# Idle transposes at the start, one product kept in PSUM, and weights moved by a graph, in a two-layer graph network

## The chip, the core and the metric

The kernel runs on one core of a Trainium2 chip. The metric is the device time of one execution in microseconds, and the median of several executions is compared. The engines are called as in the profile: PE (TensorE, matrix products), DVE (VectorE), ACT (ScalarE), POOL (GpSimd) and SP (SyncE, which here only issues DMA transfers). Each engine works through its own queue in order, and waits at an instruction until what that instruction needs is there.

## What is computed

There are 16 graphs of 1024 nodes with 256 features, one 1024x1024 adjacency matrix, and two layers:

```
# layer 0
h   = relu(layernorm(x))                    # x: 16 x 1024 x 256
A   = symmetric weights from the channel mean of h (abs, tanh)
g   = relu(einsum('bcn,bnm->bcm', h^T, adj * A) * para)
q   = g^T;  k, v = split(h @ kv_w)          # 4 heads of 64
x1  = x + softmax(q k^T * scale) v
# layer 1
h   = relu(layernorm(x1))
agg = A_hat @ h                             # normalised adjacency
y1  = relu(batchnorm(agg @ W1^T + b1))      # statistics over all 16 graphs
y2  = batchnorm(y1 @ W2^T + b2)             # the same
out = x1 + y2
```

Each batchnorm needs the statistics of all graphs before any value of it can be finished, so the program has three stages one after the other: attention of all graphs with the first product of layer 1 beside it, the second product of layer 1 for all graphs, and then the output of all graphs.

## The kernel before, in words

All data is float32. A tile is 128 partitions by some columns; a graph's 1024 nodes are 8 tiles (`NT`), its 256 features are 2 chunks (`CC`). In the part that runs, `layers(False)`, the order of the instructions on each engine is the order in which the program issues them (`layers(True)`, a version with shifted exponents for extreme inputs, is built too and not run here). That order is written with Python generators: `weave` takes one step of a main sequence and then one of each side sequence, `islice` takes so many steps, `double` takes two steps at a time. `run` works a sequence to its end.

**The start** (lines 1179 to 1200). `load_x(0)` (line 173) fetches graph 0 in two transfers of 512 KB on SP's queue; behind them stand the key and value weights (`kvw`) and the first pieces of the adjacency matrix (`load_adj`). `Norm` makes h tile by tile: statistics on DVE, the reciprocal root on POOL, a shift on DVE, then one ACT instruction per tile (`relu`, line 341). `transposed` (line 385) turns four tiles of h for one feature chunk into a PSUM bank with four PE transposes, and ACT copies the bank out (line 399). `keys_values` (line 643) makes k and v from it: the `pk` products. `differences` and `weigh` make the weights w of the graph products: per piece two ACT instructions `abs` (line 480), one `tanh` (line 488), and one multiplication with adj on DVE (line 467). `plain_queries` are the graph products (`pg`). All of these PSUM banks come in turn from one pool of three (`bank`, line 164).

**The attention stage** (`attention`, line 1086) is a loop of steps. A step issues the scores of two node tiles (`sc`, 8 PE instructions, into one of two PSUM buffers each), ACT makes their exponentials p (line 935), DVE adds these up (`acc`), and one step later PE multiplies p with v (`o`). Between these, PE gets background work: `background(b)` yields pieces with a cost, and a step takes pieces until `done` reaches `due`. The background of graph b's attention makes keys, values and queries of graph b+1, and the aggregation and hidden product of graph b-1. The weights of graph 2 are begun in graph 0's background, in `prepare(2, ...)` (lines 811 to 816): for each of two feature chunks up to three slots of `weigh` (an even slot is a multiplication of the piece before and the `abs` of the next, an odd slot is a `tanh`), beside v products, then the transposes of that chunk. Graph 1's background then goes on with them: one slot beside each of four `pk` products (line 852), then two slots beside each product of `queries(2)` (line 855).

**The second product** (`second`, line 1208). `graph(b, ...)` (line 1333) makes the product of graph b in seven block products of 4 PE instructions each (`m1` to `m7`, line 1328), which ACT and DVE combine into two tiles `y2_b_0` and `y2_b_1` that stay in SBUF to the end. `ahead_of(b + 1)` is taken between them: relu of the next graph's input on ACT, the combinations t1 and t2 on POOL, and the load of the input after that. The pair t1, t2 lies in the tile `both` for the first and last graph, else in the tags of `y2_15`. Between graphs `load_x1` (line 1243) fetches x1 of graph 0, 1, 2, ..., as far as there is room: three in the pool `xp`, four in the input buffers `yin`, one in `both`, so eight.

**The output** (lines 1444 to 1469). Per graph: ACT applies the batchnorm's scale and shift, 32 PE transposes turn y2 into rows (`pt`), DVE adds them onto x1 (line 1464), POOL issues two DMA writes of 512 KB, and one more x1 is fetched: graphs 8 to 10 into the tiles y2_0 to y2_2 whose turn is over, the others into buffers of earlier x1, which come free when their output has been written.

Of the kernel before, what the change touches and what calls it, by code (L numbers as in the profile page):

```python
# [10 lines left out]
F32 = mybir.dt.float32  # L11
# [12 lines left out]
def gnn_two_layers_kernel(  # L24
# [72 lines left out]
    def layers(shifted):  # L97
# [74 lines left out]

        def load_x(b):
            xs[b] = p3.tile([P, NT, C], F32, tag="x", name=f"x_{b}")
            for half in range(2):
                t = slice(half * NT // 2, (half + 1) * NT // 2)
                nc.sync.dma_start(
                    out=xs[b][:, t], in_=x[b].rearrange("(t p) c -> p t c", p=P)[:, t]
                )
# [202 lines left out]

        TOP = -1.0

        def transposed(b, k, halves=range(NH)):

            h = hs["a", b]
            if 0 in halves:
                ht = p3.tile([P, N], F32, tag="ht", name=f"ht_{b}_{k}")
                hts.setdefault(b, []).append(ht)  # L390
            ht = hts[b][k]
            for g in halves:
                pt = bank(f"htp_{b}_{k}_{g}")
                for j in range(FB // P):
                    t = g * (FB // P) + j
                    nc.tensor.transpose(
                        pt[:, j * P : (j + 1) * P], h[:, t, k * P : (k + 1) * P], ident
                    )
                nc.scalar.copy(ht[:, g * FB : (g + 1) * FB], pt)  # L399

        def squares(b):

# [86 lines left out]
                yield 0.0  # L489

        AHEAD = 6

        def quarters(tag, b):

# [311 lines left out]
        def prepare(b, products):  # L806


            w = weighers[b]
            yield from islice(products, 1)  # L810
            if b == 2:
                for k in range(CC):
                    yield from weave(islice(products, 3), (0, islice(w, AHEAD // 2)))
                    yield TOP
                    transposed(b, k)
# [13 lines left out]
        def background(b):  # L829

            if b == 0:
                differences(1)
                for k in range(CC):
                    yield TOP
                    transposed(1, k)
# [12 lines left out]
            before = hidden(b - 1)  # L848
            gather = aggregate(b - 1)
            if b + 1 < B:  # L850
                w, products, norm = weighers[b + 1], keys_values(b + 1), normed(b - 1)
                yield from weave(islice(products, 4), (0, islice(w, 4)))
                if b == 1:
                    load_later()
                yield from weave(queries(b + 1), (0, double(w)), (9, islice(norm, 5)))
                yield next(gather)
                yield from weave(products, (0, norm))
            else:
                yield from weave(endings.pop(), (2, normed(b - 1)))
# [295 lines left out]
        with st:  # L1155
            if shifted:
                for b in range(B):
                    if b > 0:
                        load_x(b)
                    run(Norm(b, True).all())  # L1160
                    differences(b)
                    for k in range(CC):
                        transposed(b, k)
                    run(islice(weighers[b], AHEAD))
                    run(weave(plain_queries(b), (0, weighers[b])))
                    if b == 0:
                        run(degrees(), graph())
                        load_later()
                    run(keys_values(b))
                    shifted_attention(b)  # L1170
                    norm = Norm(b, False)
                    run(norm.all())
                    keep(b)
                    if b == B - 1:
                        attn.close()
                        turns.append(second(kind))
                    run(aggregate(b), hidden(b))
            else:
                norm = Norm(0, True)
                norm.stats(0, 1)  # L1180
                norm.scale(0, 2)
                for t in range(2, NT, 2):
                    norm.stats(t, t + 1)
                    norm.shift(t - 2, 2)
                    norm.relu(t - 2, t - 1)
                    norm.scale(t, 2)
                norm.shift(NT - 2, 2)
                norm.relu(NT - 2, NT - 1)
                products = keys_values(0)

                for k in range(CC):
                    transposed(0, k, (0,))
                run(islice(products, 2))
                for k in range(CC):
                    transposed(0, k, (1,))
                differences(0)
                run(weave(products, (0, islice(weighers[0], AHEAD))))
                load_x(1)
# [9 lines left out]
    def second(kind):  # L1208
# [34 lines left out]
        def load_x1():  # L1243


            b = len(xos)
            name = f"xo_{kind}_{b}"
            HT = NT // 2
            if not 8 <= b < 11:
                pool, tag = ((xp, "xo"), (io, "yin"), (wp, "both"))[(b % 11 > 2) + (b % 11 > 6)]  # L1250
                xo = pool.tile([P, NT, C], F32, tag=tag, name=name)
                halves = [xo[:, :HT, :], xo[:, HT:, :]]
            else:
                halves = [
                    yp.tile([P, HT, C], F32, tag=f"y2_{b - 8}_{i}", name=f"{name}_{i}")
                    for i in range(2)
                ]
            for i in range(2):
                nc.sync.dma_start(out=halves[i], in_=by_rows(x1_d[b], i))
            xos.append(halves)  # L1260

        with st:
# [34 lines left out]

            def second_steps(b):

                if 0 < b < B - 1:  # L1300
                    pair = [
                        yp.tile([P, JH, FB], F32, tag=f"y2_{B - 1}_{i}", name=f"t{i}_{kind}_{b}")
                        for i in range(2)
                    ]
                else:
# [27 lines left out]
            def graph(b, ahead):  # L1333

                b11, t3, b21, b22 = inputs(b)
                y2.append(
                    [
                        yp.tile([P, N], F32, tag=f"y2_{b}_{k}", name=f"y2_{kind}_{b}_{k}")
                        for k in range(CC)
                    ]  # L1340
                )
# [34 lines left out]
            def ahead_of(b):  # L1376
# [15 lines left out]
                        load_y(2 * b + 2 + i)  # L1392
                yield

            stats2 = wp.tile([P, CC, B * NH, 6], F32, name="stats2")
            mv2 = wp.tile([P, CC, 2], F32, name="mv2")
            affs = []
# [28 lines left out]
            yield  # L1426
            yp = st.enter_context(tc.tile_pool(name=f"yp_{kind}", bufs=1, reuse_waits="tile"))
            xp = st.enter_context(tc.tile_pool(name=f"xp_{kind}", bufs=3))
            for b in range(B):
                graph(b, ahead_of(b + 1))  # L1430
                if b in (1, 3, 5, B - 2, B - 1):
                    for _ in range(1 + b // (B - 2)):
                        load_x1()
                if kind == "f" and b == B // 2:
# [97 lines left out]
```

## Time and profile before

| | us |
|---|---|
| median of 3 runs | 2499.18 (2499.15 to 2500.88) |
| the profiled execution, its own time | 2498.36 |
| its span, first to last instruction | 2496.6 |
| PE busy | 2436.2 |
| DVE busy | 1882.5 |
| ACT busy | 1399.5 |
| POOL busy | 430.1 |

DMA moved 421.42 MB, 169 GB/s over the span. In the row of 40 slices, about 62 us each, PE stands at 8 tenths in the first, at 5 in the last and at 9 (90% or more) in all others; the last slice is also the one with the most traffic, 380 GB/s. In the profile's lines a number of a line (L171) is that of the kernel before, `a<-b` names what is written and read, and the bracket at the end tells how long the engine had idled and what ended it. "PEld" rows are weight loads that run beside the products. A PE product of float32 is recorded as two matmuls.

### The profile page before, as it was taken

What the parts mean: (1) busy time and instruction counts of PE and PEld (TensorE: products, weight loads), DVE (VectorE), ACT (ScalarE), POOL (GpSimd) and SP (SyncE); (2) the same over time, 40 slices, a digit from 0 to 9 for tenths busy, and PEclk for the clock granted to TensorE, in tenths of its full rate; (3) what the DMA queues carried; (4) which work ended last, traced back from release to release, by engine and by line L of the source; (5) the groups of instructions that cost most, each with busy time, mean ns of one, the idle gap of its engine ahead of it and who ended that gap; (6) DMA issues with size and microseconds to landing.
All of it is one profiled execution on the core that took longest, in us unless ns stands there. A gap on an engine that the chain in (4) does not pass through costs nothing. (4 is left out here: it accounts for less than half of the span.)

```text
span 2496.6 us, 35488 instructions
## 1 busy us (share of the span) xinstructions
PE 2436.2 (98%) x13363; PEld 838.4 (34%) x13363; DVE 1882.5 (75%) x2919; ACT 1399.5 (56%) x1924; POOL 430.1 (17%) x527
## 2 busy tenths in 40 slices
PE   8999999999999999999999999999999999999995
PEld 3333333333333333333333333333333332334444
DVE  4668787877778787878787787868787877757775
ACT  6775554647474645656464747465564634345554
POOL 1550101010101001010101010110101001136652
PEclk9999999999999999999999999999999999999997
DMA  4654535354554445362645445444535334355459
GB/s 144 220 194 150 188 96 206 113 193 133 183 159 177 157 162 171 111 210 83 215 126 182 144 173 169 177 152 142 179 111 203 105 140 169 127 211 223 181 195 380
DMA packets 187877, 421.42 MB, mean 169 GB/s; under 512 B 21800, under 2 KB 81712, under 8 KB 181936
## 3 DMA queue, kind: packets, MB, share of 16 engines
q1 hardware_dynamic: 158528, 311.56, 37.1%
q0 software_dynamic: 29168, 107.50, 11.6%
q8 instruction: 108, 1.77, 0.3%
q14 instruction: 73, 0.60, 0.1%
HBM read 315.63 MB, written 103.35 MB: 168 GB/s over the span
## 5 line engine op out<-in xcount | busy, mean ns | idle before, releaser
L935 ACT ACTIVATE p<-sc 128x1024 f32<-128x1024 f32 x512 | 495.2, 1019 | 620.8 <-PE sc L927 620.3
L959 DVE TENSOR_TENSOR acc<-acc,p 128x1024 f32<-128x1024 f32 x384 | 472.7, 1231 | 165.8 <-ACT p L935 144.1
L927 PE MATMUL sc<-q,k 64*64 64x512 f32 x4096 | 499.8, 603 | 4.6 <-ACT p L935 4.6
L970 PE MATMUL o<-p,v 128*64 128x512 f32 x2048 | 494.6, 604 | 0.3 <-DVE os L984 0.3
L171 PE MATMUL pg<-w,h_a 128*64 128x512 f32 x1600 | 359.8, 592 | 0.4 <-DVE w L467 0.4
L171 PE MATMUL pa<-aht,h_b 128*64 128x512 f32 x1536 | 346.2, 592 | 3.8 <-ACT h_b L341 3.8
L480 ACT ACTIVATE w<-cbc,csum 128x512 f32<-128x512 f32 x256 | 285.7, 1168 | 0.0
L927 PEld LDWEIGHTS sc<-q,k 64*64 64x64 f32 x4096 | 131.2, 132 | 346.4 <-issue 285.9
L467 DVE SCALAR_TENSOR_TENSOR w<-w,adj 128x1024 f32<-128x1024 f32 x128 | 156.2, 1221 | 100.0 <-ACT w L488 96.5
L171 PE MATMUL py<-at,w 128*64 128x512 f32 x1024 | 228.2, 592 | 0.2 <-ACT y L767 0.2
L970 PEld LDWEIGHTS o<-p,v 128*64 128x64 f32 x2048 | 124.5, 136 | 298.2 <-issue 260.2
L988 POOL DMA_DIRECT2D out_d<-os x58 | 34.2, 589 | 1078.6 <-DVE os L984 1045.2
L171 PEld LDWEIGHTS pg<-w,h_a 128*64 128x64 f32 x1600 | 114.9, 137 | 228.6 <-issue 217.8
L171 PEld LDWEIGHTS pa<-aht,h_b 128*64 128x64 f32 x1536 | 110.0, 137 | 218.1 <-issue 202.4
L767 ACT ACTIVATE y<-py,vec 128x512 f32<-128x512 f32 x128 | 87.4, 683 | 113.9 <-PE py L171 89.2
L488 ACT ACTIVATE w<-w 128x1024 f32<-128x1024 f32 x128 | 135.1, 1055 | 1.7
L542 DVE TENSOR_TENSOR w<-w,w 128x1024 f32<-128x1024 f32 x112 | 132.6, 1214 | 1.5
L768 POOL DMA_DIRECT2D y_d<-y x128 | 69.4, 542 | 367.9 <-ACT y L767 358.7
L171 PEld LDWEIGHTS py<-at,w 128*64 128x64 f32 x1024 | 74.2, 137 | 145.4 <-issue 131.1
L171 PE MATMUL pk<-ht,kvw_f 128*64 128x512 f32 x512 | 118.0, 604 | 1.5 <-ACT ht L399 1.5
L171 PE MATMUL pv<-kvw_f,ht 128*64 128x256 f32 x1024 | 116.1, 379 | 0.0
L341 ACT ACTIVATE h_b<-x,lnsm_b 128x256 f32<-128x256 f32 x128 | 69.9, 600 | 66.0 <-DVE lnsm_b L330 66.0
(162 smaller groups left out, 2654.5 us busy)
## 6 DMA issues: line engine op xcount, KB each, us to landing
aht<-aht_d SPq DMA_DIRECT2D x224, 512.0 KB, 6.1
adj<-in_adj_dram SPq DMA_DIRECT2D x128, 512.0 KB, 4.9
y_d<-y POOLq DMA_DIRECT2D x128, 256.0 KB, 3.3
yin_f<-y_d SPq DMA_DIRECT2D x32, 1024.0 KB, 6.3
x<-in_x_dram SPq DMA_DIRECT2D x32, 512.0 KB, 5.2
para<-in_para_dram SPq DMA_DIRECT2D x64, 256.0 KB, 3.8
x_d<-x POOLq DMA_DIRECT2D x16, 1024.0 KB, 5.1
xo_f<-x_d SPq DMA_DIRECT2D x32, 512.0 KB, 8.3
```

Source lines behind the costliest of these rows:

```text
L171: nc.tensor.matmul(dst[r], left[:, r], right, start=start, stop=stop)
L341: nc.scalar.activation(self.h[:, t, :], self.src[:, t, :], AF.Relu, bias=self.sm[:, 1, t : t + 1], scale=self.sm[:, 0, t : t + 1], accum_o ...
L467: nc.vector.scalar_tensor_tensor(w, w, 1.0, a, op0=ALU.add, op1=ALU.mult)
L480: nc.scalar.activation(w[:, t, :].rearrange("p (t q) -> p t q", q=P), cbc[:, q * NT // NH : (q + 1) * NT // NH], AF.Abs, bias=csum[:, th * ...
L488: nc.scalar.activation(made[i], made[i], AF.Tanh, scale=-0.5 / C)
L542: nc.vector.tensor_sub(block(i)[part], block(x)[part], block(y)[part])
L767: nc.scalar.activation(y, made, AF.Identity, bias=b1[:, j : j + 1])
L768: nc.gpsimd.dma_start(out=y1_d[i][:, j, :], in_=y)
L927: nc.tensor.matmul(sc[part, e, :], ks[b][k][r, m * P + c * HW : m * P + (c + 1) * HW], qs[b][k][r, f * FB : (f + 1) * FB], start=True, sto ...
L935: nc.scalar.activation(pr, sc, AF.Exp)
L959: nc.vector.tensor_add(self.acc, self.acc, pr)
L970: nc.tensor.matmul(self.o[r, :], vs[b][k][:, m, r], pr[:, e, :], start=(m == 0), stop=(m == NT - 1),)
```

## The change

Four things change, with no change of what is computed.

1. `load_x(0)` is issued as four transfers of 256 KB.
2. 28 transposes of the identity matrix into an unused bank are issued as PE's first instructions. The first-half transposes of graph 0 move to the middle of the norm loop, for both feature chunks together, with three more idle transposes after each pair; their copies so stand on ACT's queue between the fourth and fifth tile's relu. The second-half transposes are interleaved over the chunks too.
3. In `prepare(2, ...)` each chunk takes two slots instead of three; graph 1's background takes two slots beside each of the first three `pk` products instead of one beside each of four.
4. In the second product, t1 and t2 get tags of their own (`t_0`, `t_1`). Graph 12's result is made in the place of y2_15, copied by ACT to a PSUM tile (four banks) right after, and read from there for its output. `both` is free after graph 0, so it takes x1 of graph 3 after graph 7; x1 of graph 8 goes to the t tags after graph 15, and x1 of graph 9 to 15 into y2_0 to y2_6.

```diff
         def load_x(b):
             xs[b] = p3.tile([P, NT, C], F32, tag="x", name=f"x_{b}")
-            for half in range(2):
-                t = slice(half * NT // 2, (half + 1) * NT // 2)
+            parts = 4 if b == 0 else 2
+            for part in range(parts):
+                t = slice(part * NT // parts, (part + 1) * NT // parts)
...
+        def transposed(b, ks, halves=range(NH), meanwhile=None):
...
             for g in halves:
-                pt = bank(f"htp_{b}_{k}_{g}")
+                pts = [bank(f"htp_{b}_{k}_{g}") for k in ks]
                 for j in range(FB // P):
                     t = g * (FB // P) + j
-                    nc.tensor.transpose(
-                        pt[:, j * P : (j + 1) * P], h[:, t, k * P : (k + 1) * P], ident
-                    )
-                nc.scalar.copy(ht[:, g * FB : (g + 1) * FB], pt)
+                    for k, pt in zip(ks, pts):
+                        nc.tensor.transpose(
+                            pt[:, j * P : (j + 1) * P], h[:, t, k * P : (k + 1) * P], ident
+                        )
+                    if meanwhile is not None:
+                        meanwhile()
+                for k, pt in zip(ks, pts):
+                    nc.scalar.copy(hts[b][k][:, g * FB : (g + 1) * FB], pt)
...
+        IDLE = 28
...
-                    yield from weave(islice(products, 3), (0, islice(w, AHEAD // 2)))
+                    yield from weave(islice(products, 3), (0, islice(w, AHEAD // 3)))
...
-                yield from weave(islice(products, 4), (0, islice(w, 4)))
+                ahead = islice(w, 4) if b > 1 else double(islice(w, AHEAD))
+                yield from weave(islice(products, 4), (0, ahead))
...
+                idle = bank("idle")
+
+                def turn_idly(n):
+                    for i in range(n):
+                        nc.tensor.transpose(idle[:, i % NS * P : (i % NS + 1) * P], ident, ident)
+
+                turn_idly(IDLE)
                 norm = Norm(0, True)
...
                     norm.scale(t, 2)
+                    if t == NT // 2:
+                        transposed(0, range(CC), (0,), lambda: turn_idly(3))
...
-                for k in range(CC):
-                    transposed(0, k, (0,))
                 run(islice(products, 2))
-                for k in range(CC):
-                    transposed(0, k, (1,))
+                transposed(0, range(CC), (1,))
...
-            if not 8 <= b < 11:
-                pool, tag = ((xp, "xo"), (io, "yin"), (wp, "both"))[(b % 11 > 2) + (b % 11 > 6)]
+            if b < 8:
+                pool, tag = ((xp, "xo"), (wp, "both"), (io, "yin"))[(b > 2) + (b > 3)]
...
+                tag = f"y2_{b - 9}" if b > 8 else "t"
...
-                if 0 < b < B - 1:
+                if b > 0:
                     pair = [
-                        yp.tile([P, JH, FB], F32, tag=f"y2_{B - 1}_{i}", name=f"t{i}_{kind}_{b}")
+                        yp.tile([P, JH, FB], F32, tag=f"t_{i}", name=f"t{i}_{kind}_{b}")
...
+                tag = f"y2_{B - 1 if b == HELD else b}"
...
+            HELD = B - 4
...
+            ps_held = st.enter_context(tc.tile_pool(name=f"ps_held_{kind}", bufs=1, space=PSUM))
             for b in range(B):
                 graph(b, ahead_of(b + 1))
-                if b in (1, 3, 5, B - 2, B - 1):
+                if b == HELD:
+                    for k in range(CC):
+                        held = ps_held.tile([P, N], F32, name=f"held_{kind}_{k}")
+                        nc.scalar.copy(held, y2[b][k])
+                        y2[b][k] = held
+                if b in (1, 3, 5, 7, B - 2, B - 1):
...
-            while len(xos) < min(8, B):
-                load_x1()
+            load_x1()
...
-                        y = y2[b][k][:, n]
-                        nc.scalar.activation(y, y, AF.Identity, bias=sh2, scale=s2)
+                        y = y2[b][k]
+                        if b == HELD:
+                            y2[b][k] = yp.tile([P, N], F32, tag=f"y2_7_{k}", name=f"y3_{kind}_{k}")
+                        nc.scalar.activation(
+                            y2[b][k][:, n], y[:, n], AF.Identity, bias=sh2, scale=s2
+                        )
```

More of the change, by code (lines that the diff above doesn't have):

```diff
@@ L383, in layers @@
         TOP = -1.0
-        def transposed(b, k, halves=range(NH)):
+        def transposed(b, ks, halves=range(NH), meanwhile=None):
             h = hs["a", b]
[L388 to L391, printed above, removed]
+            for k in ks:
+                if 0 in halves:
+                    ht = p3.tile([P, N], F32, tag="ht", name=f"ht_{b}_{k}")
+                    hts.setdefault(b, []).append(ht)
             for g in halves:
-                pt = bank(f"htp_{b}_{k}_{g}")
+                pts = [bank(f"htp_{b}_{k}_{g}") for k in ks]
                 for j in range(FB // P):
                     t = g * (FB // P) + j
-                    nc.tensor.transpose(
-                        pt[:, j * P : (j + 1) * P], h[:, t, k * P : (k + 1) * P], ident
-                    )
-                nc.scalar.copy(ht[:, g * FB : (g + 1) * FB], pt)
+                    for k, pt in zip(ks, pts):
[6 more added lines that the diff above has]
+                    nc.scalar.copy(hts[b][k][:, g * FB : (g + 1) * FB], pt)
         def squares(b):
@@ L812, in prepare @@
                 for k in range(CC):
-                    yield from weave(islice(products, 3), (0, islice(w, AHEAD // 2)))
+                    yield from weave(islice(products, 3), (0, islice(w, AHEAD // 3)))
                     yield TOP
-                    transposed(b, k)
+                    transposed(b, (k,))
                     yield 1.0
@@ L834, in background @@
                     yield TOP
-                    transposed(1, k)
+                    transposed(1, (k,))
                     yield 1.0
@@ L1162, in layers @@
                     for k in range(CC):
-                        transposed(b, k)
+                        transposed(b, (k,))
                     run(islice(weighers[b], AHEAD))
@@ L1253, in load_x1 @@
             else:
+                tag = f"y2_{b - 9}" if b > 8 else "t"
                 halves = [
-                    yp.tile([P, HT, C], F32, tag=f"y2_{b - 8}_{i}", name=f"{name}_{i}")
+                    yp.tile([P, HT, C], F32, tag=f"{tag}_{i}", name=f"{name}_{i}")
                     for i in range(2)
@@ L1335, in graph @@
                 b11, t3, b21, b22 = inputs(b)
+                tag = f"y2_{B - 1 if b == HELD else b}"
                 y2.append(
                     [
-                        yp.tile([P, N], F32, tag=f"y2_{b}_{k}", name=f"y2_{kind}_{b}_{k}")
+                        yp.tile([P, N], F32, tag=f"{tag}_{k}", name=f"y2_{kind}_{b}_{k}")
                         for k in range(CC)
```

## The prediction

> **What bounds the kernel now.** I read the busy times first, then the waits of PE, then the stretches in which PE waits, then the end.
>
> ```profile
> PE 2436.2 (98%) x13363; PEld 838.4 (34%) x13363; DVE 1882.5 (75%) x2919; ACT 1399.5 (56%) x1924; POOL 430.1 (17%) x527
> ```
>
> PE is the bound: 60.4 us of the span of 2496.6 are not its. So only what touches a wait of PE, a slow PE, or the end after PE counts. The view of waits names PE's waits (total, times, longest):
>
> ```profile
> PE htp L396 <- ACT h_a L341: 8.6, 1, 8.6
> ...
> PE sc L927 <- ACT p L935: 4.6, 5, 2.5
> ```
>
> The first is the start (1.5 more for `pk` follow there), the second holds 2.47 + 0.49 us where graph 2's weights begin. The timeline of the start (start, duration, what):
>
> ```profile
> 5.23 0.75 DVE L317 BATCH_NORM_STATS2 st_a<-x 128x6 f32<-128x256 f32 x2 [5.23 <-DMA x<-in_x_dram]
> ...
> 13.18 6.38 PE L171 MATMUL pk<-ht,kvw_f 128*64 128x512 f32 x16 [1.48 <-ACT ht L399]
> ...
> 21.41 3.65 PE L171 MATMUL pk<-ht,kvw_f 128*64 128x512 f32 x16
> ```
>
> The same sixteen records take 6.38 us at 13.18 and 3.65 at 21.41: PE starts at half clock, and the first clock record (full speed) stands at 18.72. The columns of the next view are busy times, then clock and DMA:
>
> ```profile
> 2425.10:2428.50 3.40, 3.40 (x17) 3.01 (x16) 2.37 (x4) 3.40 (x5) 0.63 (x1) 0.50 0.03 10
> 2428.50:2431.90 3.40, 3.33 (x26) 3.14 (x27) 3.26 (x6) 3.40 (x4) 1.17 (x3) 1.00 0.96 296
> ...
> 2440.00:2450.00 10.00, 10.00 (x71) 9.32 (x70) 10.00 (x18) 10.00 (x10) 2.13 (x4) 1.00 1.03 418
> ```
>
> From about 2431 to 2491 the DMA engines are full at 418 GB/s while PE, DVE and ACT run out of work (PE has none from 2470 on): the end is bound by bytes. The third slow place is ACT's; an `abs` pair (161.46, 2.34) stands ahead of the first of these rows:
>
> ```profile
> 163.71 1.91 ACT L935 ACTIVATE p<-sc 128x1024 f32<-128x1024 f32 x2
> ...
> 164.76 3.02 PE L927 MATMUL sc<-q,k 64*64 64x512 f32 x16 [2.47 <-ACT p L935]
> ...
> 171.84 2.00 PE L927 MATMUL sc<-q,k 64*64 64x512 f32 x16 [0.49 <-ACT p L935]
> ```
>
> **The start, part 1 and 2.** SP issues each transfer in some 0.5 us; two more push `kvw` and adj back by 1 us. `kvw` landed at 8.06 and is wanted after 10; nothing else waits for SP there. The bytes of the first half transfer were complete at 4.59, of its first quarter at 3.90, so statistics start 0.68 sooner. The second pair of tiles, which came after the first pair (6.12), can start when quarter two lands, about 5.23: 0.89 sooner. DVE then makes two statistics, three small reductions of constants and the shift, 1.58 us as before (6.12 to 7.70), so the first relu moves from 7.88 to 7.0. Relus come every 0.585 us: the fourth ends at 9.35. Before, both copies waited for all eight relus; now they stand behind four. With PE ready at once the copy starts near 9.8 instead of 12.56, and `pk` at 9.8 + 0.62 (13.18 - 12.56) = 10.4. The other four relus (to 13.2) lie beside `pk`.
>
> PE's idle transposes start when the identity is there (1.3) and take 0.213 us each at half clock (spacing of the `pt` rows in 2425 to 2428), 0.12 at full: at most 6 us, done by 7.4, before the first relu ends at 7.6. They delay nothing. At full clock a tile's five transposes take 0.55 to 0.6 us, the pace of the relus.
>
> Whether they lift the clock decides part 2. [...] The rows of 2425 to 2432 speak against it: PE does nothing but transposes there, and the clock goes from 0.50 to 1.00. I take the row. By it the two first `pk` products take 8 x 0.43 = 3.44 us: 10.4 to 13.9. Then, as before, second-half transposes, k copy, ht copies, next `pk`: 1.92 us before (19.49 to 21.41), some 0.25 more now since the interleaved banks finish together. So `pk` of 21.41 comes at 16.1: **-5.3 us**. [...] All later work of this part waits for PE or for what follows from it, so the gain stays.
>
> **The weights, part 3.** Nothing is removed. One `abs` pair (2.37) moves from beside the first chunk to beside the second, and an `abs` pair and a `tanh` (2.37 + 1.06) from there into graph 1's attention. So ahead of the scores at 164.76 one `abs` goes: p starts at 161.46, scores at 162.5, which also removes the half clock that followed (records at 165.50 to 168.91 show 0.50; the scores took 3.02 for 1.95, the transposes after them 1.65 for 1.09). ACT then makes `abs`, `tanh` (to 167.6) and the next p; PE's next scores start at 168.6 instead of 171.84, after a wait of 1.3. That would be -3.2, but the moved work is only later. ACT's list from 157.57 to the p of 196.08 holds the same instructions in both programs, and its two pauses (0.84 and 1.13 us) follow PE in the same way. So this p comes at 196.1 again, and the scores behind it at 197.15 instead of 199.17 (gain 2.0). Then DVE:
>
> ```profile
> 203.18 0.69 DVE L552 TENSOR_TENSOR h_a<-h_a 128x512 f32<-128x512 f32 x1
> ...
> 204.65 3.60 PE L171 MATMUL pg<-w,h_a 128*64 128x512 f32 x16
> ```
>
> DVE works without a pause from this p (197.12) to the end of L552 at 203.87, and that releases the fourth graph product: at 203.9 again, instead of 204.65: **-0.75**. Queued behind a late p on ACT are `abs`/`tanh` and k copies; these I followed through: the largest PE waits left are 1.3, 1.1 and 1.3 us. Bounds: -4.6 if ACT and DVE were not the limit (2.47 + 0.49 + 1.07 + 0.56), +1.7 if one of these waits brings a half clock for a 3.41 us window (a PE idle of 2.47 did at 165.50; 1.64 us at 2223.68 did not). SP's adj loads follow DVE's release by 1.5 us later, and arrive 5 us after issue, ahead of use.
>
> **The second product, part 4.** Copies: two of 128x1024; the nearest rows are `tanh` and p, 1.02 to 1.06 us.
>
> ```profile
> 2384.09 0.69 ACT L1350 ACTIVATE y_f<-m_f,vec 128x512 f32<-128x512 f32 x1 [4.63 <-PE m_f L1328]
> ...
> 2387.59 0.69 DVE L1355 TENSOR_TENSOR y_f<-m_f,y_f 128x512 f32<-128x512 f32 x1 [2.33 <-PE m_f L1328]
> ```
>
> The copy to PSUM waits for DVE's last addition (2383.86 to 2384.53 in such a graph), so m1's activation, behind it on ACT, ends near 2386.2 instead of 2384.8. Who waits for that is DVE's addition at 2387.59: hidden by 1.4 us. The relus behind it lose 0.7, and had that much before t2's combination. Cost 0; without the cover 1.5 us once. Early x1 of graph 3 falls into a stage at half DMA load: 0.
>
> What it brings is at the end: nine instead of eight x1 are there when the output starts, so the full stretch has 1.05 MB less of some 25.2: 1.05 / 0.418 = **-2.5 us**. The other fetches wait only for y2 tiles instead of written outputs; with the engines full this orders bytes and removes none. Bounds 0 to -4.
>
> **Sum:** 5.3 + 0.75 + 2.5 = 8.6 us. The profiled execution took 2498.36 (span 2496.6 and 1.8 around it), which gives 2489.8; it lies 0.8 below the median, from which the same sum gives **2490.6**.
>
> **Rivals.**
> - The weights gain in full (-4.6): for it, PE's view of waits; against it, the equal ACT list. 2499.2 - 12.4 = 2486.8.
> - Transposes do not lift the clock: start -1.0. 2499.2 - 4.3 = 2494.9. Against it, 2428.50.
> - The early fetch is hidden anyway (the start of the output or POOL's issue of the writes sets the end): no -2.5. 2493.1. For it, 4 us of nearly idle DMA at 2426 to 2430; against it, 60 us of full DMA after that.
> - Slower: ACT's backlog after 176 us. If p there came late by the whole 3.4 us moved, [...] each costing 3.4 + 1.7 us less the 2 to 3 gained ahead; about four such, 12 us net, give 2499.2 - 7.8 + 12 = 2503. It decides when waits together pass 7.8 us. Against it: the same list of ACT work.
>
> **How the numbers follow.** 0.60 for the forecast, 0.14, 0.13 and 0.09 for the first three rivals, 0.04 for the last. The range 2486.5 to 2494.5 holds the forecast, the first and third rival, and the part-lit start. A measurement tells 0.2% (5 us) from no change. Faster: 0.60 + 0.14 + 0.09 + a quarter of the second rival = 0.86; same 0.11; slower 0.03.
>
> **What would show it.** First `pk` at 10 to 11 us at 0.43 us pace; the `pk` after the second transposes near 16; no half clock near 165; a `pg` wait for DVE near 199 (all 5.3 earlier); DMA full up to a last landing 2.5 us nearer its start. A first `pk` at 0.86 pace, waits over 2 us after graph 1's first scores, or an end not set by bytes would make it wrong.

## The result and the profile after

| | before | after |
|---|---|---|
| median, us (runs) | 2499.40 (8; 2498.38 to 2500.88) | 2492.72 (8; 2491.11 to 2492.97) |
| ratio, 95% interval | | 0.9971 (0.9961 to 0.998) |
| profiled execution, us | 2498.36 | 2492.90 |
| its span, us | 2496.6 | 2491.1 |

The change takes away 6.7 us, where 8.6 were forecast. The page's row of busy times after:

```profile
PE 2437.8 (98%) x13403; PEld 842.0 (34%) x13403; DVE 1880.2 (75%) x2919; ACT 1401.8 (56%) x1926; POOL 428.0 (17%) x527
```

PE has 40 more instructions, the 28 idle transposes at its start and twelve among the first tiles; ACT has the two copies. PE is still the bound, so again only its waits, its clock and the end count. The start in the timeline after (start, duration, what, and in brackets the idle time before it):

```profile
1.39 5.51 PE L1190 MATMUL idle<-ident 128*128 128x128 f32 x28 [1.39 <-POOL ident masks.py:199]
...
4.53 0.75 DVE L318 BATCH_NORM_STATS2 st_a<-x 128x6 f32<-128x256 f32 x2 [4.53 <-DMA x<-in_x_dram]
...
10.70 3.65 PE L171 MATMUL pk<-ht,kvw_f 128*64 128x512 f32 x16 [0.24 <-ACT ht L404]
...
16.53 3.65 PE L171 MATMUL pk<-ht,kvw_f 128*64 128x512 f32 x16
```

The first sixteen `pk` records now take the 3.65 us that only the second sixteen took before, and these stand at 16.53 instead of 21.41. Further on, the same view has two places where the start's gain and the weights' gain are decided:

```profile
50.72 1.22 DVE L472 SCALAR_TENSOR_TENSOR w<-w,adj 128x1024 f32<-128x1024 f32 x1
...
51.99 2.37 PE L171 MATMUL pg<-w,h_a 128*64 128x512 f32 x10 [0.87 <-DVE w L472]
...
158.17 2.00 PE L934 MATMUL sc<-q,k 64*64 64x512 f32 x16 [0.25 <-ACT p L942]
...
164.33 2.00 PE L934 MATMUL sc<-q,k 64*64 64x512 f32 x16 [1.15 <-ACT p L942]
...
193.05 2.00 PE L934 MATMUL sc<-q,k 64*64 64x512 f32 x16 [0.95 <-ACT p L942]
...
199.09 0.69 DVE L558 TENSOR_TENSOR h_a<-h_a 128x512 f32<-128x512 f32 x1
...
199.93 3.65 PE L171 MATMUL pg<-w,h_a 128*64 128x512 f32 x16 [1.18 <-DVE h_a L558]
```

At 51.99 PE waits 0.87 for DVE (0.35 before). The wait of 2.47 us ahead of the third graph's weights is gone; several of about 1 us stand in its place, and the last one is the forecast wait of `pg` for DVE. The view of PE's waits after (total, times, longest):

```profile
PE sc L934 <- ACT p L942: 4.3, 7, 1.1
...
PE pg L171 <- DVE h_a L558: 1.2, 1, 1.2
PE htp L398 <- ACT h_a L342: 1.0, 1, 1.0
PE pg L171 <- DVE w L472: 0.9, 1, 0.9
```

8.6 us of waiting for the first relu have become 1.0 (the idle transposes fill most of the rest; the relu itself starts at 7.20 instead of 7.88), while the scores wait nearly as long in all as before (4.3 after 4.6), in seven pieces instead of five. And there is one place that the change doesn't touch. In the table of stretches after (PE, PEld, DVE, ACT, POOL busy, granted clock, DMA share, GB/s) the aggregation of graph 14 has half clock:

```profile
2091.60:2095.00 3.40, 3.32 (x24) 0.77 (x16) 3.05 (x5) 2.25 (x3) 2.16 (x4) 1.00 0.85 313
2095.00:2098.40 3.40, 0.72 (x4) 0.34 (x6) 3.37 (x12) 1.37 (x3) 0.00 (x0) 1.00 1.13 278
2098.40:2101.80 3.40, 3.40 (x14) 0.79 (x14) 0.39 (x3) 2.18 (x5) 1.25 (x2) 0.50 0.73 266
```

The same place before:

```profile
2097.40:2100.80 3.40, 2.18 (x12) 0.48 (x8) 3.09 (x5) 1.46 (x2) 1.30 (x3) 1.00 0.92 343
2100.80:2104.30 3.50, 1.96 (x12) 0.57 (x16) 2.29 (x11) 2.07 (x4) 1.00 (x2) 1.00 1.09 291
```

PE waits there 2.77 us for a relu of ACT before and 2.76 after. The stretches are cut, rounded, in steps of 3.413 us from the clock's records: the shortest half-clock record of both traces lasts 3.413 us, and of the others all but each trace's last are whole multiples of it (2252.796 us is 660). Before, the wait lay across two such stretches, 1.2 and 1.5 us of idle in each, and the record shows full clock throughout. After, 2.7 us of it lay in one, and the next stretch is recorded at half clock.

Landmarks of the two profiled executions give the account (us from the start). It compares one execution with one; what of it is the change and what is chance, the experiments tell.

| | before | after | difference | gain of this stretch |
|---|---|---|---|---|
| second sixteen `pk` | 21.41 | 16.53 | -4.88 | 4.88 |
| first scores | 59.94 | 55.58 | -4.36 | -0.52 |
| fourth `pg` of graph 2 | 204.65 | 199.93 | -4.72 | 0.36 |
| first output transpose | 2423.55 | 2420.53 | -3.02 | -1.70 |
| last output landed | 2492.91 | 2487.45 | -5.46 | 2.44 |

### The profile page after: what moved, and what is told of

It reads as the page before. It is cut to its first block, busy times and chain, and to the rows that moved or that the text cites. A ratio compares the mean times of both kernels' runs of the same rounds, so it can differ in the third digit from the quotient of the medians.

```text
span 2491.1 us, 35563 instructions
## 1 busy us (share of the span) xinstructions
PE 2437.8 (98%) x13403; PEld 842.0 (34%) x13403; DVE 1880.2 (75%) x2919; ACT 1401.8 (56%) x1926; POOL 428.0 (17%) x527
```

## The experiments

Medians are of each kernel's runs, and every ratio is to the kernel before on the same chip. Differences under 1 us between medians of different groups are within what these groups scatter, so small terms are read from landmarks.

### Each part alone

On the kernel before: parts 1 and 2 alone, part 3 alone, part 4 alone. The fourth kernel is the one after without the idle transposes. The diffs, cut to one place each:

```diff
# parts 1 and 2
+                        transposed(0, range(CC), (0,), lambda: turn_idly(3))
# part 3
-                    yield from weave(islice(products, 3), (0, islice(w, AHEAD // 2)))
+                    yield from weave(islice(products, 3), (0, islice(w, AHEAD // 3)))
# part 4
+                        nc.scalar.copy(held, y2[b][k])
# after without idle transposes
-                turn_idly(IDLE)
...
-                        transposed(0, range(CC), (0,), lambda: turn_idly(3))
+                        transposed(0, range(CC), (0,))
```

> The kernel before with parts 1 and 2 alone (four transfers, idle transposes, first-half transposes among the tiles). Theory: the pk behind the second-half transposes comes at 16.5 us instead of 21.4 as in the changed kernel (-4.9), and 0.5 us of it is lost at the last graph products of graph 0, whose weights wait for an adjacency transfer behind the loads of graphs 1 and 2; so about -4.4 us. Rival (prediction's value, nothing lost behind): -5.3. Rival (transposes don't lift the clock): about -1.

> The kernel before with part 3 alone. Theory (the time is only lent: ACT's and DVE's work up to graph 1's fourth graph product is the same): PE's 2.47 us wait goes, three new waits near 1 us come, the product pg that waits for h_a comes some 0.4 to 0.8 us earlier, and the time falls by that: -0.4 to -0.8. Rival (the waits of PE named in the profile are gained in full): -3 to -4.6. Rival (the backlog costs): slower by 1 or more.

> The kernel before with part 4 alone (graph 12's product in PSUM, nine x1 fetched ahead). Theory: last write lands 2.4 to 2.5 us nearer to the first output transpose (1.05 MB at 418 GB/s); graph 13 shows no wait of PE behind the two copies; -2.4. Rival (hidden anyway): 0. Rival (copies hold ACT up): PE waits about 1.5 us once, -1.

> The changed kernel without any idle transpose; the order of all else is kept. Theory (transposes lift PE's clock): first pk still near 10.7 us but at 0.85 us pace, [...] so 1.7 to 3.4 us more than the changed kernel, 2.6 in the middle: about 2495.3. Rival ([...] the gain of the start is the order alone): no difference from the changed kernel, 2492.7.

| | median (runs) | before (runs) | ratio (95%) |
|---|---|---|---|
| parts 1, 2 | 2495.25 (18) | 2499.65 (48) | 0.9982 (0.9975 to 0.9989) |
| part 3 | 2499.00 (13) | 2499.65 (48) | 0.9998 (0.999 to 1.0006) |
| part 4 | 2496.66 (13) | 2499.65 (48) | 0.9989 (0.9981 to 0.9997) |
| after without idle transposes | 2494.41 (15) | 2499.65 (48) | 0.998 (0.9972 to 0.9987) |

The start is worth 4.4 us, the weights 0.65 with an interval that holds zero, the output 3.0. The landmarks of the profiled executions, each less the one of before, scatter little in the last two columns and more in the first two:

| gain over before, us | start to second `pk` | from it to first scores | scores to fourth `pg` | output to its last landing |
|---|---|---|---|---|
| parts 1, 2 | 5.30 | -0.52 | 0.02 | -0.14 |
| part 3 | 0.88 | -0.28 | 0.35 | -0.24 |
| part 4 | 0.64 | -0.49 | 0.02 | 2.64 |
| after | 4.88 | -0.52 | 0.36 | 2.44 |

The -0.14 and -0.24 at the output belong to parts with no edit there: so much does that landmark scatter.

*The start of before is not one number.* Parts 3 and 4 change nothing ahead of the first scores, and yet their executions reach the second `pk` 0.88 and 0.64 sooner than the profiled execution of before. What differs is when the clock reached full speed: at 18.72 in before, at 16.89 and 17.36 in these two, and the first sixteen `pk` records took 6.38, 5.46 and 5.68 us. So the 5.30 is counted from the slowest of three such starts. And what stands as -0.52 behind it is no loss of the new start, for the wait ahead of a late `pg` is there with the old start too. Before:

```profile
56.36 3.65 PE L171 MATMUL pg<-w,h_a 128*64 128x512 f32 x16 [0.35 <-DVE w L467]
```

With part 4 alone:

```profile
56.21 3.65 PE L171 MATMUL pg<-w,h_a 128*64 128x512 f32 x16 [0.84 <-DVE w L467]
```

Part 3 alone has 0.64 there. Against these two the kernel with parts 1 and 2 is 4.4 and 4.7 us ahead at the second `pk` and still 4.2 and 4.6 ahead at the first scores; the medians say 4.4.

*The idle transposes.* In the timeline of the kernel without them:

```profile
10.64 6.39 PE L171 MATMUL pk<-ht,kvw_f 128*64 128x512 f32 x16 [0.46 <-ACT ht L404]
```

`pk` starts as early as with them, at 10.64 against 10.70, and takes 6.39 us instead of 3.65. So the quarter transfers and the interleaved order bring the early start, and the idle transposes bring its pace: 2.7 us at the second `pk` (19.21 against 16.53), 2.7 still at the first output transpose, and 1.4 to 2.1 by medians (5.2 under its kernel before, where the kernel after is 6.7 and in its repeat 7.3 under).

*The wait that part 3 removes.* The kernel with part 4 alone keeps the old order of weights. Its PE timeline:

```profile
164.60 2.00 PE L927 MATMUL sc<-q,k 64*64 64x512 f32 x16 [2.48 <-ACT p L935]
...
171.68 2.00 PE L927 MATMUL sc<-q,k 64*64 64x512 f32 x16 [2.07 <-ACT p L935]
```

and the stretches there, cut in steps of 3.41 us from that execution's first clock record (17.36):

```profile
160.72:164.13 3.41, 1.40 (x8) 0.24 (x4) 2.53 (x3) 3.41 (x4) 3.25 (x5) 1.00 0.74 229
164.13:167.55 3.42, 2.95 (x24) 1.27 (x25) 2.59 (x3) 3.42 (x6) 0.39 (x1) 1.00 0.63 193
```

Here a cut falls inside the wait of 2.48 us, 2.01 us of idle lie in the first stretch, and the clock did not halve: the scores take 2.00, not 3.02. Yet the next scores stand at 171.68 and not much ahead of before's 171.84, because ACT's p is not ready: the wait in front is 2.07 instead of 0.49. So the half clock at 165.50, which the prediction counts among what part 3 removes, cost nothing by itself. ACT's list sets the time of this stretch.

*The copies.* ACT in the same kernel:

```profile
2383.12 1.02 ACT L1438 COPY held_f<-y_f 128x1024 f32<-128x1024 f32 x1 [2.15 <-DVE y_f L1367]
2386.04 1.02 ACT L1438 COPY held_f<-y_f 128x1024 f32<-128x1024 f32 x1 [1.90 <-DVE y_f L1374]
2386.99 0.68 ACT L1352 ACTIVATE y_f<-m_f,vec 128x512 f32<-128x512 f32 x1
```

They take 1.02 us each and push an activation back, and PE has no wait from 2360 to 2399. They cost nothing.

*The ninth x1.* What DMA moves from the first output transpose to the end, before:

```profile
DMA packets 7116, 25.96 MB, mean 353 GB/s; under 512 B 800, under 2 KB 800, under 8 KB 7102
...
xo_f<-x_d SPq DMA_DIRECT2D x16, 512.0 KB, 11.2
```

and after:

```profile
DMA packets 6839, 24.96 MB, mean 326 GB/s; under 512 B 768, under 2 KB 768, under 8 KB 6825
...
xo_f<-x_d SPq DMA_DIRECT2D x14, 512.0 KB, 16.0
```

One x1 (two transfers) is gone from a stretch in which DMA runs at some 418 GB/s: 1.05 / 0.418 = 2.5 us. From the first output transpose to the last landing, the eight profiled executions with part 4 and the same output code take 66.73 to 67.03 us, the three without part 4 69.36 to 69.60. Part 4 also lets the other fetches wait for y2 tiles instead of written outputs; that was not run apart, and the bytes alone account for 2.5 of the 2.6 between the means.

### What took the rest: the half clock at one wait, the transfers of x

Four kernels on one chip: the one after again; after with eighteen idle transposes ahead of graph 14's aggregation; after with forty in PE's wait for the last norm's scale; after with x of graph 2 requested behind graph 0's pieces of the adjacency instead of ahead of them.

```diff
# eighteen transposes
+            if b == B - 2:
+                warm = bank(f"warm_{b}")
+                for i in range(WARM_PA):
+                    nc.tensor.transpose(warm[:, i % NS * P : (i % NS + 1) * P], ident, ident)
# forty transposes: the same loop ahead of
             scales(1)
# x of graph 2 later
                 load_x(1)
+                products, norm = plain_queries(0), Norm(1, True).all()
+                run(weave(islice(products, 11), (0, weighers[0]), (5, norm)))
                 load_x(2)
-                run(weave(plain_queries(0), (0, weighers[0]), (5, Norm(1, True).all())))
+                run(weave(products, (0, norm)))
```

> The changed kernel again, beside the same runs of the kernel before as the next three. The parts alone gave -4.4, -0.65 and -3.0, together -8.0. Theory (the parts add up, [...]): 2491.5 to 2492, with runs in two groups some 1.6 us apart. Rival (the parts take something from each other): 2492.7 again.

> The changed kernel with 18 idle transposes ahead of graph 14's aggregation, in PE's wait of 2.76 us for h. Theory ([...]): no half-clock record near 2098, the upper group of runs goes, and the median falls by 0.8 to 1.6 against the changed kernel. Rival (the half clock there is hidden by a wait of ACT or DVE, as the one near 165 us was): the record goes and the time stays. Rival (transposes delay the product): slower.

> The changed kernel with 40 idle transposes in the 5.2 us in which PE waits for the scale of the last batchnorm. Theory (the first output transposes at half clock delay the first write and the first fetch that waits for y2_0): no half-clock record at 2419, the first write is issued 1 to 1.5 us sooner, and the end, which is bound by bytes from then on, comes 1 to 1.5 us sooner. Rival (the nine fetches ahead still hold the DMA engines then): 0 to 0.3. Rival (the idle transposes are not done when y2 is ready): slower by up to 1.

> The changed kernel with graph 2's input fetched after the adjacency pieces of graph 0's weights instead of ahead of the last five. Theory (1 MB of graph 2's input stands ahead of the adjacency pieces on a full DMA, and graph 0's last weights wait for these): PE's wait of 0.87 us near 51 goes, -0.5 to -0.9. Rival (the wait is DVE's own work): 0.

| | median (6 runs each) | lowest to highest | ratio to before (95%) |
|---|---|---|---|
| after again | 2492.22 | 2490.74 to 2493.19 | 0.9971 (0.9959 to 0.9983) |
| transposes at the aggregation | 2490.84 | 2490.57 to 2491.38 | 0.9966 (0.9954 to 0.9978) |
| transposes at the output | 2491.61 | 2490.41 to 2493.61 | 0.997 (0.9958 to 0.9982) |
| x of graph 2 later | 2491.42 | 2489.92 to 2492.17 | 0.9967 (0.9955 to 0.9979) |

*The repeat.* It was expected at 2491.5 to 2492, with runs in two groups some 1.6 us apart. It came at 2492.22, and its six runs show no two groups. The profiled executions show the half clock itself. Eleven of the thirteen executions are of kernels that leave the wait of 2.76 us at graph 14's aggregation as it is. Seven of them have the half clock there (after and its repeat, part 3, part 4, no idle transposes, x of graph 2 later, more weights moved), four do not (before, parts 1 and 2, forty transposes at the output, x in two transfers). From the fourth `pg` to the first output transpose the seven take 2220.41 to 2220.61 us and the four 2218.90 to 2218.97. So the half clock costs 1.4 to 1.7 us, and it comes with the execution, not with the change.

*Aggregation.* The timeline with the eighteen transposes:

```profile
2094.19 2.19 PE L734 MATMUL warm<-ident 128*128 128x128 f32 x18
...
2097.03 1.94 PE L172 MATMUL pa<-aht,h_b 128*64 128x512 f32 x8 [0.65 <-ACT h_b L343]
```

`pa` takes 1.94 us instead of 3.03, and no clock record of this execution shows half speed there. The median is 1.4 us lower and the six runs lie within 0.8 us instead of 2.45. The intervals against before overlap, so the size is read from the traces (1.4 to 1.7, above; this one takes 2218.97) and the runs only agree with it.

*The adjacency.* After, SP issues the first transfer of this group at 24.19, and the piece that DVE waits for, behind x of graphs 1 and 2, lands 13.13 us later (37.32); DMA moved 370 GB/s from 26.5 to 38. Before it was 12.61 (29.07 to 41.68), but with part 3 or part 4 alone, and so with the old start, 12.90 and 13.11. With x of graph 2 behind these pieces, PE's timeline has one unbroken row up to the scores:

```profile
39.48 14.76 PE L171 MATMUL pg<-w,h_a 128*64 128x512 f32 x68
54.17 1.95 PE L934 MATMUL sc<-q,k 64*64 64x512 f32 x16
```

The wait of 0.80 that stands in that row in the repeat of the kernel after (at 51.49) is gone, the scores come at 54.17 instead of 55.07, and the median is 0.8 lower. So the order of the requests makes this wait; the change neither made nor removed it.

*Output.* The forty transposes ended too early. Stretches of that execution, cut at its half-clock record (2420.66):

```profile
2417.25:2420.66 3.41, 1.85 (x14) 1.42 (x12) 1.18 (x7) 2.26 (x4) 0.81 (x2) 1.00 0.94 375
2420.66:2424.07 3.41, 3.13 (x16) 2.56 (x15) 2.77 (x4) 3.41 (x5) 0.63 (x1) 0.50 0.12 48
```

Two waits of 0.80 and 0.76 around the first output transposes left 1.56 us of idle in the first of these stretches, with nothing but transposes in the rest of it, and the second is recorded at half clock. It was put off, not removed. Of the 1 to 1.5 us expected, the output gained 0.3 (66.62 after 66.92). The median is 0.6 lower, but this profiled execution also lacks the half clock at the aggregation, so the rest is not shown to come from these transposes.

### Sizes of the two moves, and the best version

After with x of graph 0 in two transfers, as before; after with more of graph 2's weights moved into graph 1's attention (one slot per chunk, eight slots ahead); and the gains put together: x of graph 2 later, the eighteen transposes, and at the output 46 transposes ahead of the scale and 5 more behind the first output transpose.

```diff
# two transfers
-            parts = 4 if b == 0 else 2
+            parts = 2
# more weights moved
-                    yield from weave(islice(products, 3), (0, islice(w, AHEAD // 3)))
+                    yield from weave(islice(products, 3), (0, islice(w, AHEAD // 6)))
...
-                ahead = islice(w, 4) if b > 1 else double(islice(w, AHEAD))
+                ahead = islice(w, 4) if b > 1 else double(islice(w, AHEAD + 2))
# together, beside the two edits shown above
+            turn_warm(46)
             scales(1)
...
+                                if b == half == g == j == k == 0:
+                                    turn_warm(5)
```

> The changed kernel with graph 0's input in two transfers again. Theory: statistics of the first tiles start 0.7 us later, the first relu 0.7 to 0.9 later, and the first pk with it, all kept to the end: +0.7 against the changed kernel (2492.2). Rival (the clock or ACT decides the start): 0.

> The changed kernel with one slot instead of two for graph 2's weights beside each chunk of graph 0's background, and the two left out beside graph 1's pk products (eight slots instead of six). Theory (ACT and DVE have the same list up to the scores' exponential ahead of graph 1's second pg wait, so time is only lent): PE's waits near 157 and 163 shrink, those near 182 and 192 grow, the pg that waits for h_a starts at the same distance from the first pk within 0.4 us, and the time is within 0.5 us of the changed kernel. Rival (each slot moved out is a gain): -2 or more. Rival (backlog): slower by over 1.

> The changed kernel with graph 2's input fetched late, 18 idle transposes ahead of graph 14's aggregation, and 46 + 5 in the wait for the last batchnorm's scale and after the first output transpose. The first two gave -0.8 and -1.4 alone; the third, with 40 alone, left 1.6 us of PE idle in one window and the clock fell, -0.3 by the trace. Theory: the parts add, and with under 1 us idle the clock now stays up for the output: 2492.2 - 0.8 - 1.4 - 1 = 2489.0. Rival (the clock falls again, or bytes set the end anyway): 2489.7 to 2490.

| | median (runs) | before (runs) | ratio (95%) |
|---|---|---|---|
| x in two transfers | 2493.62 (13) | 2499.36 (33) | 0.9977 (0.9969 to 0.9986) |
| more weights moved | 2494.35 (21) | 2499.36 (33) | 0.998 (0.9973 to 0.9987) |
| together | 2489.35 (5) | 2499.36 (33) | 0.996 (0.9946 to 0.9974) |

*Two transfers.* The second `pk` stands at 17.27 (16.10 in the repeat of the kernel after), the scores at 56.07 (55.07): against the first execution of the kernel after (16.53 and 55.58) it is 0.7 and 0.5. So the quarters are worth 0.5 to 1.0 us at the scores, and 0.9 to 1.6 by medians, each against its kernel before; 0.7 was expected. The first relu starts at 7.88 to 7.93 in the four profiled executions with halves and at 6.56 to 7.20 in the nine with quarters, 0.7 to 1.4 sooner, where 0.89 had been worked out from the landing of the quarters.

*More weights moved.* This was to change little. From the first scores to the fourth `pg` of graph 2 it takes 146.26 us, where the nine executions with part 3 as it is take 144.33 to 144.37: it costs 1.9 us (1.7 to 2.3 by medians, each against its kernel before). PE's timeline:

```profile
194.15 2.95 PE L934 MATMUL sc<-q,k 64*64 64x512 f32 x16 [3.75 <-ACT p L942]
```

A wait of 3.75 us, and half clock after it: the scores take 2.95 us instead of 2.00. ACT's own waits from 145 to 200 (total, times, longest) in that kernel:

```profile
ACT p L942 <- PE sc L934: 1.7, 2, 1.3
ACT os L987 <- PE o L977: 1.4, 1, 1.4
```

and in the kernel after:

```profile
ACT os L987 <- PE o L977: 0.8, 1, 0.8
ACT p L942 <- PE sc L934: 0.5, 1, 0.5
```

With fewer weights beside the first chunks ACT runs dry and waits for PE 1.8 us longer in these two rows. Its list is the same, so all behind that is later, until PE waits for it at once. That is the mechanism of the prediction's slower rival at one of the scores, reached by going further in the change's own direction. "The same list, so the same end" holds only while ACT has no more pauses than before.

*Together.* The last kernel is 10.0 us under before, where the repeat of the kernel after, on another chip, is 7.3 under. Its median of 2489.35 lies between what was expected if the clock stays up (2489.0) and if it falls again (2489.7 to 2490). Its stretches at the output:

```profile
2416.00:2420.00 4.00, 3.50 (x27) 2.83 (x25) 1.69 (x9) 3.05 (x5) 0.81 (x2) 1.00 0.80 326
2420.00:2424.00 4.00, 3.19 (x22) 2.81 (x23) 2.90 (x5) 4.00 (x4) 1.18 (x2) 1.00 0.39 62
```

The clock stays full through the first output tiles, the first write is issued 3.39 us after the first output transpose (3.94 in the repeat of the kernel after), and the output takes 66.13 us instead of 66.92. Its five runs lie within 0.32 us. It has one half-clock record of its own, at 2219.06 in the second product, and that cost nothing: from the fourth `pg` to the first output transpose it takes 2218.96 us.

## Why the prediction was right, and where it was off

The direction and the main mechanisms were right, and the time is 2.1 us from the forecast. By its steps:

- **Start, to the second `pk`: right, with a size that leaned on one execution.** The first `pk` was to come at 10.4 at 0.43 us pace and came at 10.70 (10.27 in the repeat) in 3.65 us for the sixteen records; the second was to come at 16.1 and came at 16.53 (16.10). But the 21.41 from which -5.3 was counted belongs to an execution whose clock rose late (18.72); two others with the same start had 20.53 and 20.77, so the gain of the kernel after and its repeat is 4.0 to 5.3 by the pair that is compared; by medians parts 1 and 2 bring 4.4. The prediction took the time at which the clock rose in one profile for a property of the program.
- **Transposes and the clock: the row was right.** After, PE did nothing but transposes from 1.39 on, and the clock records show full speed from 6.01; without the idle ones `pk` ran at 0.80 us a product (6.39 us for sixteen records). The rival's start of -1.0, the author's estimate, is refuted.
- **"All later work ... so the gain stays": not contradicted.** The 0.52 that seems lost at 52 us is a wait for the adjacency that three executions with the old start have too, as 0.35, 0.64 and 0.84. Against the last two of these, all of the gain but 0.0 to 0.2 is still there at the first scores.
- **Weights: the right mechanism, a term mis-sized.** -0.75 forecast, -0.36 measured (first scores to fourth `pg`: 144.35 after 144.71; 144.36 with part 3 alone, and 144.69 with parts 1 and 2 or part 4 alone). The limit was named rightly: ACT's list, then DVE, and `pg` waits for L558 as forecast. But DVE's end was taken as unmoved at 203.87. Counted from the first scores it came 0.28 later (199.79 - 55.58 against 203.87 - 59.94), and `pg` started 0.14 behind it. 0.27 of the 0.28 is already there at ACT's p (196.08 before, 191.99 after), with the same pauses of 0.84 and 1.13 us: the list holds the same instructions, but in another order they take longer. An `abs` pair followed by the `tanh` that reads it takes 2.38 to 2.45 us to that instruction's start, one followed by a p or a `k` copy 2.25 or 2.26 (161.46 to 163.71); before has three of the latter up to this p, after none (a `k` copy behind a p gives 0.2 back). That the half clock at 165.50 was hidden showed in the kernel with part 4 alone.
- **Second product: right.** The copies cost nothing, and the output took 69.36 and takes 66.92: -2.44 against -2.5 (-2.64 alone), with 1.0 MB less moved in it.
- **Not foreseen: the half clock at graph 14's aggregation.** 1.7 us of the profiled execution. The change doesn't touch that place; behind the same wait the one profile of before kept full clock, as three others of the eleven did, and the kernels with part 3 or part 4 alone got half clock. The prediction again read one profile's clock as the program's.

5.3 + 0.75 + 2.5 became 4.36 + 0.36 + 2.44 = 7.2 in the profiled executions without the half clock's 1.7, against 6.7 by medians (7.3 in the repeat), which agrees within the scatter of the medians. That the medians do not show the 1.7 fits the seven of eleven, if before loses it about as often as the others; its one profile can't show how often. Of the 2.1 us between forecast and median, the start's late clock makes some 0.9 (5.3 against 4.4), the weights 0.4 and the median of before 0.2 (2499.18, then 2499.40); the other 0.6 is within the scatter.

The rivals: transposes that don't lift the clock fell with the first `pk` (3.65 us) and with the kernel without them (6.39). An early fetch that is hidden fell with part 4 alone. The weights' gain in full fell with part 3 alone. ACT's backlog did not come at the size that was moved, and came at the next size.

## What to carry to other kernels

One profile shows one draw of the clock: the same start took 5.46 to 6.38 us for its first products in three executions, so count a gain from several. Where DMA engines are full (here 370 GB/s), order the requests by who waits first: here that took 0.9 us away at the scores. A half clock or a long wait is worth only what the next engine's list leaves of it: look at the next instruction of the same kind before counting it, and when moving background work off an engine, ask where that engine then runs dry. Half clock behind waits of PE such as those here was a chance and not a fact (2.76 us: in seven of eleven executions; 2.5 us ahead of graph 1's scores, with the old order of weights: in two of three): fill such a wait with idle work, which here took 1.4 us off the median, or read several executions before counting its clock.

## What the runs showed of the hardware

- **The clock's records began at another time in each execution, and the same wait had two outcomes.** Full speed is first recorded at 6.01 and 4.30 in two executions of the kernel after, and at 18.72, 16.89 and 17.36 in three with the old start. The wait of PE of 2.76 us at graph 14's aggregation was followed by half clock in seven of eleven executions. In the two that are cut into stretches above, the idle of one stretch was at most 1.5 us where the clock stayed (before) and 2.7 us where it halved (after).
- **Idle of PE in a stretch of 3.41 us with products in it, and the clock recorded next.** Full: 1.24 and 1.52 us (before, the aggregation), 1.95 (parts 1 and 2 alone, the same place) and 2.01 (part 4 alone, the row 160.72). Half: 2.47 (before, ahead of 165.50) and 2.71 (after, the aggregation). Parts 1 and 2 alone, near 160 us, had 2.01 us of idle too, with the busy time in fourteen records instead of eight, and half clock came next. So these runs show no amount of idle that tells the two outcomes apart; what sets the two executions with 2.01 apart stays open:

```profile
157.96:161.37 3.41, 1.40 (x14) 0.41 (x16) 2.68 (x5) 3.41 (x5) 0.00 (x0) 1.00 0.48 154
161.37:164.79 3.42, 3.42 (x22) 2.07 (x16) 2.42 (x3) 3.42 (x4) 0.00 (x0) 0.50 0.00 0
```

- **The same among transposes alone.** Half clock was recorded after 1.56 us of idle in a stretch (forty transposes at the output, the row 2417.25) and after 1.75 (before, 2459.25 to 2462.66), full clock after 1.05 (after, 6.01 to 9.42). The clock also rose there: a stretch with 3.41 us of transposes at half clock (after, 2422.65 to 2426.06) was followed by full clock. With products 1.95 and 2.01 us (above) kept full clock; why these halved with less was not shown.
- **Smaller transfers of x brought its first part sooner and its last later.** x of graph 0 in quarters of 256 KB landed first at 3.84 to 4.51 and last at 7.09 to 8.12 (nine profiled executions); in halves of 512 KB first at 5.21 to 5.26 and last at 6.71 to 7.00 (four). `kvw`, asked for next, landed at 8.46 to 9.81 instead of 8.06 to 8.36, which was still ahead of its use at the first `pk` (10.07 to 10.70 with both quarters and idle transposes).
